# Residual, output and gate transfers on GpSimd's queue, quadrant rows loaded by halves a step ahead, and a looser chain for the right operands' sums

## The chip, the cores and the metric

The kernel runs on one core of a Trainium2 chip. The metric is the device time of one execution in microseconds (us). Before the change it is 2142.83 us, the median of three runs (2140.28 to 2150.28).

The engines are named as the profile names them: PE (TensorE, the matmuls), DVE (VectorE), ACT (ScalarE), POOL (GpSimd) and SP (SyncE, which here only issues DMAs). Each engine takes its instructions strictly in order. A DMA is issued by an instruction in the queue of one engine; if that instruction has to wait, everything behind it in the same queue waits too.

## The reference

The input x has shape (4, 1024, 2048), in float32. One block of a network with modulated layer norms is computed:

```python
x = x + ga * s4_convolution(layernorm(x) * (1 + ca) + sa)
x = x + gb * ffn(layernorm(x) * (1 + cb) + sb)
# ffn(h) = h @ W.T + bias + sum over 16 experts of a rank-16 update
```

The gates and shifts (sa, ca, ga, sb, cb, gb) come from a small matmul of the conditioning vector, and the 16 low-rank updates are merged into W on the chip. What the change touches is the second line: a 4096 x 2048 by 2048 x 2048 product, with its layer norm ahead of it and its gate, bias and residual behind it.

## The kernel before, in words

**First part, 0 to some 911 us.** The convolution is done as Toeplitz matmuls, block of 128 rows by block of 128 rows (32 blocks). Its result goes to the HBM tensor `x1d` (32 blocks of 128 x 2048), and each block's mean and scale go to `ln2`. Beside it the merged weights are written to HBM as `wcd`: seven right operands, each number as a pair of float16 (high and low part).

**Second part, `Ffn`, from 911 us to the end.** Four batches `s`, each of eight row blocks, so 1024 x 2048 by 2048 x 2048. Each batch product is taken apart by Strassen-Winograd into seven products of half size, in the order `ORDER = (0, 1, 5, 2, 6, 4, 3)`; `m` is the place in that order. A product runs as eight groups in `plain` (L1107): one group fills one PSUM bank of 128 x 512 with 24 matmuls (two halves of the inner dimension, four blocks, three pairs of high and low parts). From batch 1 on, the four products in `INNER` are taken apart once more in `twice` (L1130), into seven smaller products with right operands `wid`.

**Left operands.** `quad_steps` (L797) makes one quadrant (two row blocks, 1024 columns): `load` fetches two 128 x 1024 tiles `xr` from `x1d` by SP's queue (L805), `norm` normalizes them on ACT (L811), and four `turn` steps transpose them on PE into PSUM tiles `tp` (L818) and bring them back on ACT with the modulation (L821). The pool `xr` has two places, so one quadrant is in flight. `sum_steps` adds quadrants on DVE, and `piece_steps` and `inner_steps` cut the results into float16 pairs `lf` (ACT makes the high part, L860 and L875; DVE the low part, L861 and L876).

**Right operands of the second level.** In batch 0 alone, `combine_steps` (L898) runs 16 times, four times in each of the places m = 0, 2, 3 and 4 (`CBM`). Each time it loads four 128 x 2 x 512 pieces `cbi` of `wcd` (SP, L907), adds high and low parts on POOL (`whole`, L913: tiles `cbf` a, b, c), forms four sums on DVE (L928, L934, L936, L941), and for each sum calls `out`: ACT writes the high part of `cbo` (L917), DVE the low part (L918), SP stores it to `wid` (L919). `cbo` has two places, `cbi` has four.

**Results.** `outer` (L1082) takes a finished PSUM bank into accumulators on DVE or ACT. In the products 1, 4 and 3 (`FIN`) results become final, and `finish` (L1069) is called, in product 4 twice for each group: DVE adds the gated bias to the residual tile `xo` (L1075), multiplies by the gate (L1076) and adds (L1077); SP stores `xo` to `out` (L1079); then `fetch` (L1062) loads the residual that is four places further on into the place that has just been stored (L1065). `xo` has four places. `gates` (L1045) loads the gate and the gated bias for 1024 columns, 512 KB each, by SP's queue (L1050), and `scale` multiplies the gate once (L1056).

**What sets the order.** `side` (L957) gives every one of these steps a due time in groups, 0 to 8 within a product; `tick` calls the steps that are due after each group. A scheduler then moves instructions within each engine's queue by its own estimate of the times, but each engine runs them in the order that comes out. Weights `w` (1 MB each) are loaded by SP's queue too (L786).

Of the kernel before, what the change touches and what calls it, by code (L numbers as in the profile page):

```python
# [757 lines left out]
class Ffn:  # L758
# [38 lines left out]
    def quad_steps(self, s, u, hr, hc):  # L797

        nc, k = self.nc, self.k
        xs = []  # L800

        def load():
            for rb in range(2):
                x = self.pl["xr"].tile([P, D // 2], F32, tag="xr", name="xr")
                nc.sync.dma_start(out=x, in_=k.x1d[8 * s + 4 * u + 2 * hr + rb][:, ds(1024 * hc, 1024)])  # L805
                xs.append(x)

        def norm():
            for rb, x in enumerate(xs):
                r = 8 * s + 4 * u + 2 * hr + rb  # L810
                nc.scalar.activation(x, x, AF.Identity, bias=k.ln2[:, r, 0:1], scale=k.ln2[:, r, 1:2])  # L811

        def turn(c0):
            t = self.quad(f"{hr}{hc}{u}")
            tp = k.tps.tile([P, 2, 2, P], F32, tag="t", name="tp2")
            for c in range(2):
                for rb in range(2):
                    nc.tensor.transpose(tp[:, c, rb], xs[rb][:, ds(P * (c0 + c), P)], k.ident)  # L818
            for c in range(2):
                j = HC * hc + c0 + c  # L820
                nc.scalar.activation(  # L821
                    t[:, c0 + c], tp[:, c], AF.Identity, bias=k.sb[:, j, s : s + 1], scale=k.cb[:, j, s : s + 1]
                )

        return [load, norm] + [lambda c0=c0: turn(c0) for c0 in range(0, HC, 2)]

    def sum_steps(self, i, u):
        tt = self.nc.vector.tensor_tensor
# [69 lines left out]
    def combine_steps(self, i, k):  # L898

        nc = self.nc  # L900
        tt, gt = nc.vector.tensor_tensor, nc.gpsimd.tensor_tensor
        f, src = {}, {}

        def load(*names):
            for n in names:
                t = self.pl["cb"].tile([P, 2, 512], F16, tag="i", name="cbi", bufs=CBI)
                nc.sync.dma_start(out=t, in_=self.wcd_row(i, n, k))  # L907
                src[n] = t

        def whole(tag, n):  # L910
            f[tag] = self.pl["cb"].tile([P, 512], F32, tag=f"f{tag}", name="cbf")
            t = src.pop(n)
            gt(f[tag], t[:, 0], t[:, 1], ADD)  # L913

        def out(c, t):
            hl = self.pl["cb"].tile([P, 2, 512], F16, tag="o", name="cbo", bufs=2)
            nc.scalar.copy(hl[:, 0], t)  # L917
            tt(hl[:, 1], t, hl[:, 0], SUB)  # L918
            STQ(nc).dma_start(out=self.wid[i][c - 3][:, k], in_=hl)  # L919

        def s0():
            load("11", "12")
            whole("a", "11")
            whole("b", "12")

        def s1():
            f["c"] = self.pl["cb"].tile([P, 512], F32, tag="fc", name="cbf")
            tt(f["c"], f["b"], f["a"], SUB)  # L928
            out(4, f["c"])
            load("22", "21")  # L930
            whole("c", "22")

        def s2():
            tt(f["b"], f["c"], f["b"], SUB)  # L934
            out(6, f["b"])
            tt(f["a"], f["b"], f["a"], ADD)  # L936
            out(5, f["a"])
            whole("c", "21")

        def s3():  # L940
            tt(f["c"], f["c"], f["a"], SUB)  # L941
            out(3, f["c"])

        return [s0, s1, s2, s3]

    def wcd_row(self, i, n, k):
        kh, q = int(n[0]) - 1, int(n[1]) - 1
# [1 line left out]

    def begin(self):  # L950

        q = [self.quad_steps(0, 0, 0, 0), self.quad_steps(0, 1, 0, 0), self.quad_steps(0, 0, 0, 1)]
        p = [self.piece_steps(ORDER[0], u) for u in range(2)]
        self.nextq = self.quad_steps(0, 1, 0, 1)
        return q[0] + p[0] + q[1] + q[2] + p[1] + self.nextq[:1]

    def side(self, s, m):  # L957

# [5 lines left out]
            for j, f in enumerate(fs):  # L964
                out.append((t + j // n, f))

        def quad(st, t):
            put(t, st[1:2])
            put(t + 1, st[2:], 2)

        def quads(s, todo):

            n = 8 / max(len(todo), 1)
            for j, x in enumerate(todo):
                st = self.quad_steps(s, *x)
                t = j * n
                out.append((t + 0.01 if j else 0, st[0]))
                out.append((t + n / 3, st[1]))
                out.append((t + 2 * n / 3 - 0.1, st[2]))
                out.append((t + 2 * n / 3, st[3]))  # L980
                out.append((t + n - 0.2, st[4]))
                out.append((t + n - 0.1, st[5]))

        if (s, m) == (0, 0):
            c, d = self.quad_steps(0, 0, 1, 0), self.quad_steps(0, 0, 1, 1)
            self.nextq, e = d, self.nextq
            quad(e, 0)
            put(2, c[:1])
            quad(c, 3)
            put(5, d[:1])  # L990
            put(6, d[1:2])
            put(7, d[2:4], 2)
        elif (s, m) == (0, 1):
            c, d = self.quad_steps(0, 1, 1, 0), self.quad_steps(0, 1, 1, 1)
            put(0, self.nextq[4:] + c[:1], 3)
            quad(c, 1)
            put(3, d[:1])
            quad(d, 4)
        elif s + 1 < NB:
            quads(s + 1, {  # L1000
                4: ((0, 0, 1), (1, 0, 1)), 5: ((0, 0, 0), (1, 0, 0), (0, 1, 0)), 6: ((1, 1, 0), (0, 1, 1), (1, 1, 1))
            }.get(m, ()))

        if s:
            for u in range(2):
                if m == 0:
                    put(1 + 2 * u, self.sum_steps(5, u))
                    put(6 + u, self.sum_steps(2, u))
                elif m in (3, 4):
                    put(0.5 + u, self.sum_steps(ORDER[m + 1], u))  # L1010
        elif m in (1, 3, 4):
            for u in range(2):
                put(1 + 5 * u, self.sum_steps(ORDER[m + 1], u), 2)
                if m == 1:
                    put(3.5 + 4 * u, self.sum_steps(2, u))

        if m + 1 < len(ORDER) or s + 1 < NB:
            i = ORDER[(m + 1) % len(ORDER)]
            now, then = inner(s, ORDER[m]), inner(s + (m == 6), i)
            for u in range(2):  # L1020
                st = self.inner_steps(i, u) if then else self.piece_steps(i, u)
                if then:
                    ts = [E * (p + 2) + 0.1 for p in range(7)] if now else [2, 4, 6, 6.5, 8, 9.2, 10.4]
                elif now:
                    ts = [E * (2 + (4 * u + j) // 2) + 0.1 for j in range(4)]
                else:
                    ts = [2 + 4 * u + j // 2 for j in range(4)]
                for t, f in zip(ts, st):
                    if t >= 8:
                        self.later.append((t - 8 + 0.02, f))  # L1030
                    else:
                        out.append((t, f))
        if s == 0 and m in CBM:
            n = CBM.index(m)
            for k in range(4):
                for j, f in enumerate(self.combine_steps(INNER[n], k)):
                    out.append((2 * k + (j - 1) / 2 if k or j else 0, f))
        return sorted(out, key=lambda x: x[0])

    def open_slots(self):  # L1040
# [4 lines left out]
    def gates(self, hc):  # L1045
        k = self.k
        t = self.pl["g"].tile([P, 2, 1024], F32, tag="gb", name="gb")
        for i in range(2):
            src = k.gbd[i][self.s][ds(1024 * hc, 1024)]
            self.nc.sync.dma_start(out=t[:, i], in_=src.partition_broadcast(P))  # L1050
        self.gb, self.gbias = t[:, 0], t[:, 1]
        self.raw = True

# [6 lines left out]
        return x[8 * self.s + 4 * u + 2 * hr + rb][:, ds(1024 * hc + 512 * q, 512)]  # L1060

    def fetch(self, n):  # L1062
        while self.nxo < min(n, len(self.fin)):
            x = self.pl["o"].tile([P, 512], F32, tag="o", name="xo")
            self.nc.sync.dma_start(out=x, in_=self.at(self.k.x1d, *self.fin[self.nxo]))  # L1065
            self.xo[self.nxo] = x
            self.nxo += 1

    def finish(self, key, t):  # L1069
# [6 lines left out]
        v.tensor_tensor(t, t, self.gb[:, sl], MUL)  # L1076
        v.tensor_tensor(x, x, t, ADD)  # L1077
        out = self.k.io["out"].rearrange("(r p) d -> r p d", p=P)
        STQ(self.nc).dma_start(out=self.at(out, *key), in_=x)  # L1079
        self.fetch(n + AHEAD)  # L1080

    def outer(self, i, u, rb, q, ps):  # L1082
# [108 lines left out]
    def run(self):  # L1191
        self.w0, self.ne, self.raw = 0, 0, False
        for s in range(NB):
# [5 lines left out]
            self.nxo, self.xo = 0, {}  # L1199
            for m, i in enumerate(ORDER):  # L1200
                side = self.side(s, m)
                if m == 0:
                    self.fetch(AHEAD)
                if m in (0, 6):
                    self.gates(0)
                elif m == 4:
# [17 lines left out]
BLOCK = {0: (0, 0), 1: (0, 1), 2: (1, 1)}  # L1224
BANK = {0: "x", 1: "x", 4: "y", 2: "y", 5: "z", 6: "z", 3: "z"}
CBM = (0, 2, 3, 4)
CBI = 4
FIN = {1: (("a", (0, 0)),), 4: (("a", (0, 1)), ("b", (1, 1))), 3: (("b", (1, 0)),)}
LEFT = {0: "00", 1: "01", 5: "s2", 2: "01", 6: "00", 4: "10", 3: "11"}
Q1 = ("000", "001", "010", "011", "100", "101")  # L1230
# [30 lines left out]
def net(ctx: ExitStack, tc: tile.TileContext, io):  # L1261
# [165 lines left out]

    def early():
        right.close()
        for name, bufs in (("q", 1), ("xr", 2), ("l", LR)):  # L1430
            pr[name] = pool(p2, "p2" + name, bufs, "right")

    calls = [0]
# [146 lines left out]
```

## Time and profile before

| what | value |
|---|---|
| median of three runs | 2142.83 us |
| the profiled execution, its own time | 2143.21 us |
| its span in the trace | 2141.4 us |
| granted TensorE clock, mean | 0.976 |
| second part: first matmul at, last matmul at | 910.9 us, 2135.6 us |
| one PSUM group of 24 matmuls | 5.18 us |
| DMA instructions on SP's queue in one execution: xr, xo, out, gb | 64, 128, 128, 24 |
| DMA instructions on POOL's queue | 28, all before 141 us |

The profile of an execution has a page and a trace. The page gives the busy time of each engine, the costliest groups of instructions with what ended the idle time before them, and the chain of waits that ended last. The trace answers for any stretch: busy time of each engine, the granted clock (PEclk, 1.00 is full speed), the share of time in which the DMA engines were busy, and who waited for whom. In the list of waits a line reads "engine, tile and line that waited <- engine, tile and line that it waited for: us in total, times, longest". A name such as SPq stands for the queue of an engine, where DMAs are issued.

### The profile page before, as it was taken

How to read it: one execution, taken by the hardware profiler on the slowest of the kernel's cores; microseconds unless marked ns; L12 is line 12 of the kernel's file. 1: busy time of each engine (PE TensorE's matmuls, PEld its weight loads, DVE VectorE, ACT ScalarE, POOL GpSimd, SP SyncE). 2: the span in 40 equal slices, each digit the busy share in tenths (PEclk: the TensorE clock that was granted, in tenths of full speed). 3: DMA queues.
4: the chain of work that ended last, by engine and by line, in shares of the span. 5: the costliest groups of instructions: out<-in, count | busy, mean ns of one | idle time of the engine just before them, and what ended most of it. 6: DMA issues, size and time to landing. Idle time of an engine off the chain costs nothing.

```text
span 2141.4 us, 28492 instructions
## 1 busy us (share of the span) xinstructions
PE 2019.2 (94%) x10557; PEld 968.2 (45%) x10557; DVE 1617.6 (76%) x2798; ACT 950.4 (44%) x1754; POOL 116.5 (5%) x117
## 2 busy tenths in 40 slices
PE   6898999999999999989996989999899999999998
PEld 2343444444444455544443444445444444444444
DVE  5437798888979898558976778866787857778666
ACT  1324876666766686744324442224351244412210
POOL 1020000000000000032443000000000000000000
PEclk7898999999999999999998999999999999999999
DMA  9796858888986674478767876666885667766665
GB/s 405 305 377 255 326 219 336 341 330 315 338 315 232 226 263 163 155 269 276 259 241 248 274 266 217 251 208 229 275 286 198 235 211 266 270 208 244 200 220 190
DMA packets 139129, 559.16 MB, mean 261 GB/s; under 512 B 15456, under 2 KB 15984, under 8 KB 93166
## 3 DMA queue, kind: packets, MB, share of 16 engines
q1 hardware_dynamic: 137392, 553.06, 72.0%
q10 hardware_dynamic: 526, 2.63, 0.3%
q8 instruction: 83, 1.36, 0.3%
q0 software_dynamic: 1072, 1.65, 0.2%
q14 instruction: 56, 0.46, 0.1%
HBM read 443.63 MB, written 113.65 MB: 260 GB/s over the span
## 4 chain that ended last, share of the span: by engine, by line
PE 34%; DMA 9%; DVE 5%; issue 2%; ACT 1%; POOL 1%; SPq 0%; ACTq 0%; DVEq 0%; POOLq 0%
PE f L1119 13%; PE fz L1147 8%; PE fy L1147 6%; PE fx L1147 5%; DMA out<-xo 3%; DMA wid<-cbo 2%; DMA xr<-x1d 2%; DMA xo<-x1d 2%; PE tp L818 1%; POOL cbf L913 1%; DVE cbo L918 1%; DVE e L1102 1%; DVE e L1076 1%; DVE xo L1077 1%; DVE lf L876 0%
## 5 line engine op out<-in xcount | busy, mean ns | idle before, releaser
L1119 PE MATMUL f<-w,lf 128*128 128x512 f16 x3072 | 683.1, 383 | 2.1 <-DMA w<-wcd 2.1
L1119 PEld LDWEIGHTS <-lf 128*128 128x128 f16 x3072 | 303.3, 99 | 359.0 <-issue 13.4
L676 PEld LDWEIGHTS <-hc 128*128 128x128 f16 x2304 | 212.3, 98 | 215.1 <-issue 53.4
L1147 PEld LDWEIGHTS <-lf 128*128 128x128 f16 x2016 | 197.3, 98 | 235.0 <-issue 0.7
L676 PE MATMUL ya<-kh,hc 128*128 128x512 f16 (+3 forms) x768 | 203.9, 329 | 7.0 <-ACT qs L691 6.7
L676 PE MATMUL yb<-kh,hc 128*128 128x512 f16 (+3 forms) x768 | 200.9, 326 | 1.9 <-DVE we L503 1.1
L1147 PE MATMUL fz<-w,lf 128*128 128x512 f16 x864 | 192.8, 379 | 0.4 <-DVE ca L1165 0.4
L676 PE MATMUL ya<-kh,hs 128*128 128x512 f16 (+3 forms) x768 | 189.9, 326 | 2.2 <-DVE we L503 1.2
L676 PEld LDWEIGHTS <-hs 128*128 128x128 f16 x1152 | 106.1, 98 | 111.3 <-issue 26.5
L641 ACT ACTIVATE xt<-xt,cas 128x128 f32<-128x128 f32 x448 | 141.1, 393 | 10.2 <-DVE cas L587 10.2
L811 ACT ACTIVATE xr<-xr,ln 128x1024 f32<-128x1024 f32 x64 | 79.3, 1241 | 147.8 <-DMA xr<-x1d 147.5
L1075 DVE TENSOR_TENSOR xo<-xo,gb 128x512 f32<-128x512 f32 x128 | 87.9, 703 | 69.4 <-DMA xo<-x1d 55.6
L319 PE MATMUL modps<-wm,sct 128*32 128x512 f32 x768 | 119.3, 656 | 16.2 <-DMA wm<-in_wmod 8.9
L1147 PE MATMUL fx<-w,lf 128*128 128x512 f16 x576 | 129.5, 379 | 0.0
L818 PE MATMUL tp<-ident,xr 128*128 128x128 f32 x512 | 77.8, 289 | 53.7 <-ACT xr L811 35.7
L1147 PE MATMUL fy<-w,lf 128*128 128x512 f16 x576 | 128.2, 379 | 0.0
L676 PE MATMUL ya<-kl,hc 128*128 128x512 f16 (+3 forms) x384 | 126.1, 329 | 0.0
L676 PE MATMUL ya<-kl,hs 128*128 128x512 f16 (+3 forms) x384 | 125.1, 326 | 0.0
L676 PE MATMUL yb<-kl,hc 128*128 128x512 f16 (+3 forms) x384 | 125.1, 326 | 0.0
L875 ACT CAST lf<-t 128x512 f16<-128x512 f32 x72 | 44.3, 617 | 179.5 <-PE f L1119 84.9
L913 POOL TENSOR_TENSOR cbf<-cbi 128x512 f32<-128x512 f16 x64 | 93.8, 1467 | 294.3 <-DVE xo L1075 146.1
L818 PEld LDWEIGHTS tp<-ident,xr 128*128 128x128 f32 x512 | 61.9, 147 | 77.6 <-ACT xr L811 42.3
(380 smaller groups left out, 2765.8 us busy)
## 6 DMA issues: line engine op xcount, KB each, us to landing
w<-wcd SPq DMA_DIRECT2D x100, 1024.0 KB
wm<-in_wmod SPq DMA_DIRECT2D x96, 1024.0 KB
w<-wid SPq DMA_DIRECT2D x48, 1024.0 KB
x<-in_x SPq DMA_DIRECT2D x32, 1024.0 KB
x1d<-y SPq DMA_DIRECT2D x32, 1024.0 KB
xr<-x1d SPq DMA_DIRECT2D x64, 512.0 KB
xo<-x1d SPq DMA_DIRECT2D x128, 256.0 KB
out<-xo SPq DMA_DIRECT2D x128, 256.0 KB
```

The lines of the kernel that those rows point to most:

```text
L319: self.last = self.nc.tensor.matmul(self.modps[32 * g : 32 * g + 32, :], self.sct[:, j].rearrange("p r b -> p (r b)"), w[:, ds(512 * g, 512)],
L641: nc.scalar.activation(xt[:, k], src, AF.Copy, scale=cas[:, k : k + 1])
L676: nc.tensor.matmul(pf[:, o:512], h, self.kf[f][z][:, ds(k0, 512 - o)], start=first, stop=(i == last and (x, z) == (1, 0)), skip_group_chec ...
L811: nc.scalar.activation(x, x, AF.Identity, bias=k.ln2[:, r, 0:1], scale=k.ln2[:, r, 1:2])
L818: nc.tensor.transpose(tp[:, c, rb], xs[rb][:, ds(P * (c0 + c), P)], k.ident)
L875: nc.scalar.copy(hl[:, :, 0, :], src)
L913: gt(f[tag], t[:, 0], t[:, 1], ADD)
L918: tt(hl[:, 1], t, hl[:, 0], SUB)
L1075: v.tensor_tensor(x, x, self.gbias[:, sl], ADD)
L1076: v.tensor_tensor(t, t, self.gb[:, sl], MUL)
L1119: nc.tensor.matmul(ps, l[:, c, x, :], w[:, c, y, :], start=(n == 0), stop=(n == 23), skip_group_check=True)
L1147: nc.tensor.matmul(ps[name], l[:, k, x, :], w[:, k, y, :], start=(first and n == 0), stop=(n == 11), skip_group_check=True,)
```

## The change

Four things change, all in `Ffn`.

1. The gate loads (`gates`), the residual loads (`fetch`) and the result stores (`finish`) are issued by POOL instead of SP. In batch 0 the first residuals are fetched at m = 1 instead of m = 0, no more than eight of them until m = 5.
2. A quadrant is handled in two halves of 512 columns: four places of 128 x 512 for `xr` instead of two of 128 x 1024, eight smaller `norm` instructions for a pair of quadrants where there were four, and each half's load is due one half's time before its norm. The due times of all quadrants are set anew.
3. `combine_steps` is split into loads and sums that are due with the combination before, and three steps after them. A fourth tile `d` holds one of the sums, the results of one step are converted two at a time (both high parts, then both low parts), and `cbo` now takes its places from the pool `o` of four, which it shares with `xo`.
4. Some due times of sums and pieces in batch 0 move.

No arithmetic is added or left out.

```diff
@@ quad_steps
-        def load():
-            for rb in range(2):
-                x = self.pl["xr"].tile([P, D // 2], F32, tag="xr", name="xr")
-                nc.sync.dma_start(out=x, in_=k.x1d[8 * s + 4 * u + 2 * hr + rb][:, ds(1024 * hc, 1024)])
+        def load(h):
+            for rb, r in enumerate(rows):
+                x = self.pl["xr"].tile([P, 512], F32, tag="xr", name="xr")
+                nc.sync.dma_start(out=x, in_=k.x1d[r][:, ds(1024 * hc + 512 * h, 512)])
...
-        return [load, norm] + [lambda c0=c0: turn(c0) for c0 in range(0, HC, 2)]
+        return [
+            [lambda h=h: load(h), lambda h=h: norm(h), lambda h=h: turn(h, 0), lambda h=h: turn(h, 2)] for h in range(2)
+        ]
@@ combine_steps
-        def out(c, t):
-            hl = self.pl["cb"].tile([P, 2, 512], F16, tag="o", name="cbo", bufs=2)
-            nc.scalar.copy(hl[:, 0], t)
-            tt(hl[:, 1], t, hl[:, 0], SUB)
+        def high(c):
+            hl = self.pl["o"].tile([P, 512], F32, tag="o", name="cbo").bitcast(F16)
+            hl = hl.rearrange("p (y n) -> p y n", y=2)
+            nc.scalar.copy(hl[:, 0], f[WHERE[c]])
+            f[c] = hl
+        def low(c):
+            hl = f[c]
+            tt(hl[:, 1], f[WHERE[c]], hl[:, 0], SUB)
             STQ(nc).dma_start(out=self.wid[i][c - 3][:, k], in_=hl)
...
+        def sums():
             whole("a", "11")
             whole("b", "12")
             whole("c", "22")
+        def first():
+            tt(new("d"), f["b"], f["a"], SUB)
+            high(4)
             tt(f["b"], f["c"], f["b"], SUB)
+            high(6)
+            low(4)
+            low(6)
+        def second():
             tt(f["a"], f["b"], f["a"], ADD)
+            high(5)
+            tt(f["d"], f["d"], f["a"], SUB)
+            high(3)
+            low(5)
+            low(3)
-        return [s0, s1, s2, s3]
+        before = [lambda: load("11", "12", "22"), lambda: load("21"), sums]
+        return before, [first, lambda: whole("d", "21"), second]
@@ side
+        def halves(hs, t, d, loaded=0):
+            for j, h in enumerate(hs):
+                if j >= loaded:
+                    add(t + (j - 1) * d, h[0])
+                add(t + j * d + 0.1, h[1])
+                add(t + (j + 0.55) * d, h[2])
+                add(t + (j + 0.9) * d, h[3])
...
+        elif s + 1 < NB and m in (4, 5, 6):
...
+            d = 4 / len(todo)
+            halves(quads(s + 1, *todo), d, d)
@@ gates, fetch, finish
-            self.nc.sync.dma_start(out=t[:, i], in_=src.partition_broadcast(P))
+            self.nc.gpsimd.dma_start(out=t[:, i], in_=src.partition_broadcast(P))
...
-            self.nc.sync.dma_start(out=x, in_=self.at(self.k.x1d, *self.fin[self.nxo]))
+            self.nc.gpsimd.dma_start(out=x, in_=self.at(self.k.x1d, *self.fin[self.nxo]))
...
-        STQ(self.nc).dma_start(out=self.at(out, *key), in_=x)
+        self.nc.gpsimd.dma_start(out=self.at(out, *key), in_=x)
@@ run
-                if m == 0:
-                    self.fetch(AHEAD)
+                self.cap = 8 if s == 0 and m < 5 else len(self.fin)
+                if (s, m) in ((0, 1), (0, 5)) or s and m == 0:
+                    self.fetch(self.nxo + AHEAD)
@@ net
-        for name, bufs in (("q", 1), ("xr", 2), ("l", LR)):
+        for name, bufs in (("q", 1), ("xr", 4), ("l", LR)):
```

## The prediction

> **What bounds the kernel now.** I read the page's first part, then PE's waits in the second part, then a table of stretches, and last the waits of the two queues that stand behind PE's waits.
>
> ```profile
> PE 2019.2 (94%) x10557; PEld 968.2 (45%) x10557; DVE 1617.6 (76%) x2798; ACT 950.4 (44%) x1754; POOL 116.5 (5%) x117
> ```
>
> PE is the bound, and the question is what it loses. From 910.9 to 2136.2 us (1225.3) it has 5088 group matmuls, at 5.18 us for 24 (the chain's long rows: 192 in 41.44), so 1098.2 us, and 464 transposes (512 less the 48 made before 911), at 0.87 us for eight, so 50.5. The rest, 76.6 us, is all that a change of this part can win. PE's waits from 820 us on:
>
> ```profile
> PE tp L818 <- ACT xr L811: 35.7, 18, 5.5
> PE tp L818 <- ACT 010_8586 L821: 14.9, 1, 14.9
> PE tp L818 <- ACT 011_8911 L821: 2.7, 1, 2.7
> PE f L1119 <- DMA w<-wcd: 2.1, 1, 2.1
> ```
>
> These make 55.4 us, and all but the last are transposes that wait for ACT. The table of stretches (start and end, length, busy time of PE and of PEld, DVE, ACT, POOL, then PEclk, DMA share, GB/s) shows where:
>
> ```profile
> 952.40:1005.00 52.60, 43.25 (x199) 21.09 (x197) 38.42 (x46) 24.97 (x42) 13.37 (x10) 0.90 0.84 281
> 1113.00:1182.00 69.00, 50.25 (x225) 24.02 (x224) 47.30 (x65) 26.92 (x48) 25.02 (x18) 0.85 0.70 244
> 1182.00:1262.00 80.00, 70.48 (x350) 35.47 (x349) 56.40 (x91) 33.20 (x53) 0.00 (x0) 0.96 0.77 263
> 1317.00:1440.00 123.00, 123.00 (x571) 55.74 (x570) 92.84 (x142) 27.73 (x46) 0.00 (x0) 1.00 0.61 212
> 1481.00:1572.00 91.00, 84.37 (x422) 43.20 (x421) 70.22 (x108) 40.05 (x66) 0.00 (x0) 0.98 0.78 264
> 1774.00:1866.00 92.00, 85.66 (x429) 43.77 (x427) 72.18 (x111) 41.26 (x68) 0.00 (x0) 0.98 0.78 261
> ```
>
> The clock is 1.00 where PE never waits (1317 to 1440) and lower in the stretches with waits, so a wait costs more than its length. I take the waits of a stretch plus PE's busy time by what PEclk lacks:
> - A, 905 to 1010 (m = 0 and 1 of batch 0): waits 11.2, clock 43.25 x 0.10 = 4.3; 15.5.
> - B, 1025 to 1182 (the right operands' sums): waits 20.8, clock 50.25 x 0.15 = 7.5, and 85.95 x 0.02 = 1.7 before 1113; 30.0.
> - C, 1182 to 1262 (the last two products of batch 0): 9.5 + 2.8 = 12.3.
> - D and E (the same of batches 1 and 2): 6.6 + 1.7 and 6.3 + 1.7; 8.3 and 8.0.
>
> Together 74.1 of the 76.6.
>
> **C, D, E: rows that come late.** SP's own waits in E:
>
> ```profile
> SPq L1065 <- DMA out<-xo: 37.7, 18, 6.5
> SPq L1079 <- DVE xo L1077: 22.7, 16, 4.5
> ```
>
> That is 60 of 92 us in which SP's queue stands at a residual load (its place is still being stored) or at a store (DVE is not done). The `xr` loads and the weights are behind it. In D it is 61 of 91, in C 52 of 80. All PE waits of these three are for the norm of `xr`, and ACT in turn waits for the load. The change takes both from SP; what remains there in E are waits of 3.5 us (L805) and 0.4 (L786). The load is now due 1.33 + 0.1 groups ahead of its norm (7.4 us) where three quadrants share a product, instead of 0.89 (4.6 us). In the chain, `xr` takes 5.7 to 8.3 us from issue to landing, for pairs of 512 KB; the halves carry half of that. 7.4 us is enough for most. Of 28.6 us I take 23 as won, and leave 5.6 for loads that meet two weights.
>
> The smaller norms cost nothing on the path: ACT needs 0.62 us for 128x512 (the cast of L875), twice that is 1.24, what one norm takes now (1241 ns). SP gets 64 `xr` issues more (0.38 us each, 24 us over 1225) and loses 280. If ACT were no longer idle half of the time, the norms would count.
>
> **B: the sums.** ACT's waits from 1100 to 1182:
>
> ```profile
> ACT cbo L917 <- DMA wid<-cbo: 27.6, 9, 4.5
> ACT cbo L917 <- DVE cbf L934: 8.1, 3, 2.8
> ```
>
> `cbo` has two places, so ACT stands until a store has landed; the eviction of `tp` that PE wants is behind it on ACT (14.9 us). POOL's sums show the pace: six rounds from 1073.22 to 1149.12, so 12.65 us a round, where the products give 41.4 / 4 = 10.4. With four places a round no longer waits for its own stores. Its longest chain is then, from the rows: two POOL sums 3.1 (1.96 apart, then 1.15), DVE 0.69, ACT 0.62, DVE 0.69, POOL 1.54, DVE twice 0.69, ACT 0.62, DVE 0.69; 9.3 us with no queueing. DVE is busy 81% between 1025 and 1113 (71.24 of 88), so I take 11. The order of the changed program still puts all 16 rounds ahead of the first eviction that PE needs late in m = 4, six groups into it: 2 x 41.4 + 31 = 114 us after m = 2 begins, for 11 rounds. At 11 us they end 7 us late, at 9.3 in time, at 12.65 25 us late, as now. With its share of clock that leaves 10 of 30: 20 won, with ends 0 and 30.
>
> **A: places shared.** In the changed order the last two `cbo` of m = 0 stand on ACT, in m = 1, behind the store of the first finished tile (and the next four behind those of tiles four and later), with norms and evictions queued behind them. The trace has no such wait. The first store lands about one group (5.18), five DVE instructions (3.4) and one store (4.5) after m = 1 begins, 13 us; PE wants the norm behind it after three groups, 15.5 us. It just holds, but if the residual comes 5 us late, PE waits for 3, and the next `cbo` waits for its predecessor's store on top. Nearest rows on either side: the 11.2 us of waits here could all go, or a 14.9 us wait like that of B could come. I take 4 won, since SP is relieved here too (16.5 + 11.9 us of its waits between 905 and 1182).
>
> **POOL's queue instead of SP's.** What POOL pays to issue and how long a transfer takes:
>
> ```profile
> kb<-kd POOLq DMA_DIRECT2D x1, 1024.0 KB, 9.6
> gsd<-rkg POOLq DMA_DIRECT2D x24, 12.0 KB, 5.1
> gm<-gsd POOLq DMA_DIRECT2D x1, 288.0 KB, 7.4
> ```
>
> Issue takes 0.51 to 0.74 us there (eight `gsd` in 4.09, `kd` 0.74). At two tiles a group, in product 4, that is 4 x 0.74 = 3.0 us of 5.18: POOL is not the bound. The landing matters more. For comparison, SP's stores and loads on the chain in D:
>
> ```profile
> 1490.71 6.82 DMA out<-xo
> 1497.55 3.75 DMA xo<-x1d
> 1515.92 3.04 DMA out<-xo
> 1518.97 3.01 DMA xo<-x1d
> ```
>
> A place of `xo` is used again after two groups in product 4, 10.36 us. A turn is a store, a load, and about 2.5 us of DVE and of queue order: with SP's 3.0 to 6.8 and 3.0 to 3.75 it is 8.5 to 13. With 5.1 twice it is 12.7, and DVE falls behind by 2.3 us every two groups, three times over, 7 us; with 7.4 twice 17.3, 21 us. PE is covered by five PSUM banks, four groups or 20.7 us: DVE already waits 55.6 us for `xo` and the PE list has nothing of it. I take 5.5, near the 12 KB row, because a separate queue doesn't stand behind 1 MB weights, and charge 2 us. The last store pays 0.4 us more to issue and lands up to 2 later: 2 us. Together 4, with ends at 0 and 70.
>
> POOL's 94 us of sums lie in the same queue as stores that wait for DVE, in m = 1 of batch 0 only; I leave that in A.
>
> The Trainium skill speaks against this move. Its page "DMA: Bandwidth & Descriptors", section "Issuing engine by pattern", gives simple loads and stores to Sync and calls the GpSimd path slower; the section "Anatomy of one DMA" has 2.0 us plus the bytes at 436 GB/s, an estimate of 2.6 us for 256 KB. No row here is that short; by it the turn would be 7.7 us and DVE would lose nothing.
>
> The page "SBUF — State Buffer", section "Who interferes with whom", says that a DVE instruction in a two-port mode locks GpSimd out of writing descriptors. The trace shows a tile instruction at that double pace only in L1056 (128x1024 in 0.75 us, twelve in this part), so by the rule at most 9 us in all.
>
> **Sum.** 23 + 20 + 4 - 4 = 43 from the profiled execution's 2143.2: 2100 us. That execution lies 0.4 above the median of the three, so the number stands for the median as well. Half a per cent, 10.7 us, is about what a measurement of this kernel can tell from no change.
>
> **Rivals.**
> - *The sums stay slow* (20%). DVE, 81% busy, sets the 12.65 us and not the stores; or ACT's wait in A takes its place. Then 23 - 4 remain: 2124 us. For it: ACT also waits for L934 (8.1). Against it: the stores are the longest wait.
> - *POOL's transfers are slow* (15%), the one that ends slower. If a store and a load of 256 KB each take 9.6 us as `kb` did, a turn is 21.7 us, DVE falls 34 us behind in each product 4, PE waits for the 13 beyond its banks, and the product after it (one tile a group, four places, 21.7 of 20.7 us) never gives the lag back: 34 less a little each batch, 25 or so x 4 = 100, less the 43 + 4 without POOL's price: some 2196. Up to about 7.4 us each nothing of this shows; from there on it decides. For it: landing rows of 5.1 to 9.6. Against it: those ran while 16 engines were near full (first slices 9 7 9 6), here the share is 0.6 to 0.8.
> - *Nothing changes* (10%): `xr` was late for the DMA engines' load (0.78 in D and E) rather than for SP, and the sums stay as they are: 2140.
>
> **Chances.** The forecast has 55%, with its own range of 2084 (B and C to E wholly won) to 2118. Faster by over 0.5%: 55 + 20 = 75%, less 1 for the upper edge; within: 10 and a little; slower: 15. For 8 in 10 the range leaves out the slow rival and the best few per cent: 2084 to 2150.
>
> **What will show it.** C to E: no PE wait on L812, SP's queue without waits on `out`. B: POOL's rounds at 11 us or less, PEclk near 1.00 between 1113 and 1182. A: ACT's waits of `cbo` on DMA `out<-xo`. POOL: store and load of `xo` near 5.5 us each. Wrong would be: DVE waits on `xo` that grow above 100 us with PE waiting for banks, or rounds still at 12 us.

## The result, and the profile after

The changed kernel takes 2274.05 us (median, 2266.6 to 2275.13) against 2145.94 us for the kernel before in the same measurement (2140.28 to 2150.28): ratio 1.0591, 95% interval 1.0554 to 1.0628. The prediction, 2100 us and at most 2150, was wrong in sign. The profiled execution took 2275.06 us, with a span of 2273.3 us and a mean granted clock of 0.954 (before 0.976).

The first part of the page (busy time and share of the span):

```profile
PE 2043.0 (90%) x10557; PEld 975.8 (43%) x10557; DVE 1626.5 (72%) x2798; ACT 963.5 (42%) x1818; POOL 266.9 (12%) x397
```

PE does the same 10557 instructions, in 23.8 us more of busy time (the lower clock), and sits idle more. PE's waits from 820 us on:

```profile
PE tp L819 <- ACT 110_9252 L823: 42.4, 3, 17.8
PE fz L1165 <- DVE cb L1180: 33.6, 3, 13.9
PE tp L819 <- ACT 100_9068 L823: 22.2, 3, 8.9
...
PE tp L819 <- ACT xr L812: 7.2, 7, 2.6
```

The whole list comes to 145.7 us, against 56.8 before. The waits for `xr` fell from 35.7 to 7.2, as the change meant. Three others, each met three times, are new. Batch 1's three stalls in the table of stretches (columns as in the prediction):

```profile
1580.00:1600.00 20.00, 10.83 (x42) 4.99 (x40) 17.36 (x29) 7.08 (x13) 6.46 (x13) 0.76 0.68 219
1620.00:1640.00 20.00, 11.18 (x51) 5.97 (x50) 16.04 (x24) 6.66 (x13) 3.80 (x7) 0.78 0.65 229
1740.00:1760.00 20.00, 6.07 (x20) 2.26 (x19) 12.46 (x21) 0.62 (x1) 0.54 (x1) 0.68 0.44 177
```

PE works 6 to 11 of 20 us there, and the clock drops to 0.68 to 0.78. The end is late too: from the last matmul to the end of the span it is 21.9 us (2251.4 to 2273.3), before 5.4. Waits (88.9 more), clock (23.8) and tail (16.5) make 129 of the 131.9 us between the spans.

Next the waits of DVE, and the wait of POOL's queue that answers to SP's in the prediction:

```profile
DVE xo L1093 <- DMA xo<-x1d: 199.4, 72, 9.1
DVE gb L1074 <- DMA gb<-gbd: 56.2, 11, 13.0
```

```profile
POOL xo L1083 <- DMA out<-xo: 365.1, 100, 9.1
```

DVE waits 199.4 us for the residual instead of 55.6. POOL stands 3.65 us on average until a store has landed, before it can load into that place; SP stood 2.06 (206.3 over 100). Yet the transfers are not long in the median. The DMA issues (last number: us from issue to landing):

```profile
xo<-x1d POOLq DMA_DIRECT2D x128, 256.0 KB, 3.6
out<-xo POOLq DMA_DIRECT2D x128, 256.0 KB, 3.9
```

How this reaches PE is seen in batch 1. POOL's timeline (start, duration, line, operation, count; in brackets the wait before and what ended it):

```profile
1530.86 1.15 POOL L1097 DMA_DIRECT2D out<-xo  x2 [108.94 <-DVE xo L1095]
...
1544.06 1.08 POOL L1097 DMA_DIRECT2D out<-xo  x2
1554.22 0.54 POOL L1083 DMA_DIRECT2D xo<-x1d  x1 [9.08 <-DMA out<-xo]
...
1591.04 1.15 POOL L1097 DMA_DIRECT2D out<-xo  x2
...
1729.93 0.54 POOL L1083 DMA_DIRECT2D xo<-x1d  x1 [7.53 <-DMA out<-xo]
...
1736.19 0.54 POOL L1068 DMA_DIRECT2D gb<-gbd  x1 [0.18 <-issue]
```

In product 4 the stores go two by two, and POOL stands 9.08 us for this pair, where the median landing is 3.9. What ran beside it: SP's timeline, and how the queues shared the 16 DMA engines from 1549 to 1553 us (packets, MB, share of the engines' time):

```profile
1542.16 2.91 SPq L786 DMA_DIRECT2D w<-wcd  x2
```

```profile
q1 hardware_dynamic: 264, 1.21, 73.3%
q0 software_dynamic: 133, 0.41, 25.7%
```

q0 carries 81.36 MB in this execution and 1.65 MB in the one before, so it is POOL's; q1 has SP's transfers. Two weights of 1 MB were issued just ahead of the pair, rows followed from 1545.55 on, and while the pair was under way SP's queue had three quarters of the engines. Two residual loads of POOL itself (issued from 1542.98 on) were also just ahead of it. DVE's timeline:

```profile
1575.98 0.69 DVE L1093 TENSOR_TENSOR xo<-xo,gb 128x512 f32<-128x512 f32 x1 [5.25 <-DMA xo<-x1d]
...
1591.26 0.69 DVE L886 TENSOR_TENSOR t<-001_8437 128x512 f32<-128x512 f32 x1
...
1744.86 0.75 DVE L1074 TENSOR_SCALAR gb<-gb,fs_i 128x1024 f32<-128x1024 f32 x1 [13.04 <-DMA gb<-gbd]
```

ACT's, and PE's:

```profile
1591.98 0.62 ACT L879 CAST lf<-t 128x512 f16<-128x512 f32 x1 [21.51 <-DVE t L886]
...
1593.22 1.00 ACT L823 ACTIVATE 100_9068<-tp,sb,cb 128x256 f32<-128x256 f32 x2
```

```profile
1594.27 0.47 PE L819 MATMUL tp<-ident,xr 128*128 128x128 f32 x1 [8.93 <-ACT 100_9068 L823]
...
1756.25 7.67 PE L1165 MATMUL fz<-w,lf 128*128 128x512 f16 x24 [13.93 <-DVE cb L1180]
```

Read from the top: DVE stands at the residual, so the sum `t` (L886), behind it on DVE, comes late; ACT's cast of `t` waits 21.5 us for it; the eviction L823 is behind the cast on ACT, and PE wants it for its next transposes. No PSUM bank of the products is in this chain. The second stall is of the same kind (ACT's cast of `u` waits 13.3 us for DVE, the eviction L823 follows it). The third is the gate: its load was issued at 1736.2, after POOL had stood 7.5 and 4.5 us at two residual loads, and was in place 8.7 us later. DVE stood 13 us at the scaling, with the additions behind it (L1180) that empty PE's banks.

### The profile page after: what moved, and what is told of

Read it like the earlier page. It is cut to its first block, busy times and chain, and to the rows that moved or that the text cites. A ratio compares the mean times of both kernels' runs of the same rounds, so it can differ in the third digit from the quotient of the medians.

```text
span 2273.3 us, 28757 instructions
## 1 busy us (share of the span) xinstructions
PE 2043.0 (90%) x10557; PEld 975.8 (43%) x10557; DVE 1626.5 (72%) x2798; ACT 963.5 (42%) x1818; POOL 266.9 (12%) x397
## 3 DMA queue, kind: packets, MB, share of 16 engines
q0 software_dynamic: 25008, 81.36, 10.3%
## 4 chain that ended last, share of the span: by engine, by line
DMA 18%; issue 17%; PE 14%; DVE 13%; POOL 3%; ACT 1%; SPq 0%; POOLq 0%; DVEq 0%; ACTq 0%
DMA out<-xo 10%; PE fz L1165 4%; DMA xo<-x1d 3%; PE fy L1165 2%; PE f L1137 2%; PE ya L676 2%; PE fx L1165 2%; DMA cbi<-wcd 2%; DVE cbo L930 1%; DMA gb<-gbd 1%; DVE e L1094 1%; POOL xo L1083 1%; DMA wid<-cbo 1%; PE yb L676 1%; DVE e L1120 1%
## 5 line engine op out<-in xcount | busy, mean ns | idle before, releaser
L1093 DVE TENSOR_TENSOR xo<-xo,gb 128x512 f32<-128x512 f32 x128 | 87.2, 690 | 221.4 <-DMA xo<-x1d 199.4
L1165 PE MATMUL fz<-w,lf 128*128 128x512 f16 x864 | 200.6, 389 | 40.8 <-DVE cb L1180 33.6
L819 PE MATMUL tp<-ident,xr 128*128 128x128 f32 x512 | 82.4, 296 | 95.1 <-ACT 110_9252 L823 42.4
L812 ACT ACTIVATE xr<-xr,ln 128x512 f32<-128x512 f32 x128 | 102.2, 812 | 133.7 <-DMA xr<-x1d 133.7
L1097 POOL DMA_DIRECT2D out<-xo x128 | 70.0, 547 | 576.5 <-DVE xo L1095 571.8
```

The costliest lines, as they stand in the source:

```text
L819: nc.tensor.transpose(tp[:, c, rb], xs[h, rb][:, ds(P * (c0 + c), P)], k.ident)
L1093: v.tensor_tensor(x, x, self.gbias[:, sl], ADD)
L1097: self.nc.gpsimd.dma_start(out=self.at(out, *key), in_=x)
L1165: nc.tensor.matmul(ps[name], l[:, k, x, :], w[:, k, y, :], start=(first and n == 0), stop=(n == 11), skip_group_check=True,)
```

## The experiments

Where no ratio is given, there is a single time and no interval; the kernel before took 2146 to 2151 us in the same measurements. Where nothing else is said, the edit is to the changed kernel.

**The queue, or the rest.** First all three transfers back on SP, then the reverse: the kernel before with nothing but the queue changed.

```diff
-            self.nc.gpsimd.dma_start(out=t[:, i], in_=src.partition_broadcast(P))
+            self.nc.sync.dma_start(out=t[:, i], in_=src.partition_broadcast(P))
...
-            self.nc.gpsimd.dma_start(out=x, in_=self.at(self.k.x1d, *self.fin[self.nxo]))
+            self.nc.sync.dma_start(out=x, in_=self.at(self.k.x1d, *self.fin[self.nxo]))
...
-        self.nc.gpsimd.dma_start(out=self.at(out, *key), in_=x)
+        self.nc.sync.dma_start(out=self.at(out, *key), in_=x)
```

> The changed kernel with residual loads, output stores and gate loads back on SP; the half quadrants, their due times and the looser chain of sums stay. Queue theory (POOL's queue takes store, wait for its landing, load, next store in one order, so DVE waits 199 us for the residual and ACT and PE behind it): the 199.4 us of DVE waits for xo fall to 60 or less, and the time is 2100 to 2150, the upper end if the rows stand behind the residual on SP again. Order theory (the new order of rows, pieces and evictions on ACT makes PE's transposes late whatever queue is used): 2230 or more, with the 95 us of PE idle ahead of the transposes still there. Sums theory (the looser chain, with its stores in the residual's four places, is what got slower): in between, with PE's waits gathered in batch 0 and none in the later batches.

Measured: 2147.69 us, ratio to before 0.9991 (0.9974 to 1.0007). SP's waits for a place ahead of a weight load, in the products that are not split in seven, first with all on SP, then in the changed kernel:

```profile
SPq L786 <- PE f L1137: 8.7, 9, 2.1
```

```profile
SPq L786 <- PE f L1137: 219.5, 42, 17.7
```

With all on SP the queue stands 194.2 us at residual loads and 217.2 at stores, and a weight of these products, held back behind them, seldom has to wait for its place as well. With these off SP, the weights are at the head of the queue early and go out as soon as PE has freed a place.

> The kernel before with only the queue changed: residual loads, output stores and gate loads on GpSimd's queue, whole quadrants, old due times and old chain of sums. Queue theory: the loss is nearly all here, 2220 to 2280, DVE waits for xo near 200 us instead of 55.6. Order theory and sums theory: the queue costs little, 2110 to 2150, DVE waits for xo under 100 us.

Measured: 2256.58 us, ratio 1.0515 (1.0481 to 1.0548). The queue alone makes 107 of the 126 us that the changed kernel loses against its version on SP, and the rest of the change is worth nothing on SP. The order theory falls: with whole quadrants and the old due times the same stalls are there. DVE's wait, and PE's longest, in the kernel with only the queue changed:

```profile
DVE xo L1075 <- DMA xo<-x1d: 151.4, 61, 8.3
```

```profile
PE tp L818 <- ACT 111_9572 L821: 43.4, 3, 14.7
```

With all on SP, PE's longest wait from 820 on, and ACT's longest for `cbo` between 1025 and 1190, are:

```profile
PE tp L819 <- ACT xr L812: 31.1, 14, 6.2
```

```profile
ACT cbo L925 <- DVE cbf L939: 37.2, 7, 8.1
```

The rows are late again, and the chain of sums now waits for DVE where it waited for stores.

**One transfer at a time.** Only the gate loads back on SP (the first pair of lines above); only the stores; only the residual loads.

> The changed kernel with only the eight gate loads back on SP. If the gate loads behind the stores are the main cause (gate theory): below 2170. Queue theory: only PE's wait of the fz groups for DVE's L1180 (33.6 us) and DVE's 56.2 us for gb go, with the clock some 40 us: 2225 to 2250, DVE waits for xo near 190 us still. Order theory: as the changed kernel but for those 33.6: about 2240.

Measured: 2226.57 us, DVE's wait for `xo` 217.2. PE's wait for L1180 halves (16.5), and no stall of it is longer than 5.3 us (13.9 in the changed kernel): having the gates on POOL costs 47 us in all. That is a net figure: SP now stands 139.7 us at the gate loads, for a gate tile that DVE still reads, with the rows behind them, and PE's wait for `xr` is 46.5 us, the largest of all runs here.

> The changed kernel with only the output stores back on SP; residual loads and gates stay on POOL. POOL still waits for a store's landing before the load that takes its place, but no store stands behind that wait. Queue theory in the strict form (it is the one order of stores and loads): DVE waits for xo fall to 100 us or less and the time to 2110 to 2190, even though SP's queue again waits for DVE at each store. If GpSimd's queue itself is the cost (a load on it lands late whatever stands ahead of it): DVE waits for xo stay above 150 us and the time above 2220.

Measured: 2217.31 us, DVE's wait 149.9. Both lie well outside what the queue theory gave (by 27 and 50 us) and just short of the other's 2220 and 150. So the one order of stores and loads on POOL is not the whole cause; that the queue itself is the cost does not follow.

> The changed kernel with only the residual loads back on SP; stores and gates stay on POOL, where nothing waits for a landing any more. Queue theory: DVE's waits for xo fall below 110 us and the time to 2140 to 2190; SP waits for the stores' landing with rows and weights behind it, as in the kernel before (206 us), perhaps longer. Contention theory: the stores on POOL land late, SP waits above 300 us, and the time stays above 2220.

Measured: 2208.03 us, DVE's wait 127.2; SP stood 500.6 us at the stores' landing. Neither theory holds in full: the time is 18 us above the one and 12 below the other, with SP's wait as contention had it. With the loads or with the stores alone on POOL, beside the gates, the loss against 2147.69 is 70 and 60 us.

**Depth and order.** Three fetched ahead instead of four; then five places instead of four.

```diff
-AHEAD = 4
+AHEAD = 3
```

> The changed kernel with the residual fetched three finishes ahead instead of four, so a load on POOL takes the place of the tile finished one step earlier, whose store was issued 2 to 8 us before, and not of the tile whose store has just been issued. Queue theory, now sharper (on one queue each tile pays its own store's landing: 365.1 us over 100 loads, 3.65 us each, plus two issues of 0.55, where product 4 gives a tile every 2.6 us): POOL's wait for out falls below 150 us, DVE's wait for xo from 199 to 110 or less, the time to 2190 to 2225 (the gates' 13.9 us stalls stay). Contention theory (a transfer on GpSimd's queue shares the DMA engines with the weights that SP no longer holds back, and lands late whatever the order): the residual, fetched a step later, comes later still, DVE's wait for xo stays at 190 us or more and the time above 2260.

Measured: 2269.99 us, POOL's wait 367.4, DVE's 207.0.

```diff
-    for name, bufs in (("q2", 1), ("c", 1), ("o", 4), ("e", 1), ("g", 1)):
+    for name, bufs in (("q2", 1), ("c", 1), ("o", 5), ("e", 1), ("g", 1)):
```

> The changed kernel with five places for the residual instead of four and still four fetched ahead: again a load takes the place of the tile finished a step earlier, but nothing is fetched later. Queue theory: as with the later fetch or better, POOL's wait for out below 150 us, DVE's for xo below 100, 2180 to 2215. Contention theory: little moves, above 2250.

Measured: 2264.2 us, POOL's wait 403.9, DVE's for `xo` 166.0, for the gate 93.8. By the numbers contention wins, but the first of the two is no test: the scheduler moves the load up until it stands directly behind the store of its own place, and from product 4 of batch 0 on POOL's order is the changed kernel's, letter for letter. (In the source, finish n fetches tile n + 3 into the place of tile n - 1, not into the place just stored; it is the scheduler that puts each load behind its own place's store, in the kernel before as well.) In the second the load still stands behind its own place's store, one place deeper; the residual is earlier and the gate later.

> Five places and the gate loads on SP, residual and stores on POOL. Queue theory: both causes are gone, what is left is the kernel before without residual on SP: PE waits for DVE-made pieces and for L1180 under 10 us together, rows no longer late: 2120 to 2150. Contention theory: the gates' share only, as with gates on SP alone, 2215 to 2235.

Measured: 2199.73 us, ratio 1.0257 (1.0236 to 1.0277). With the gates away, the fifth place gives 27 us (against the single 2226.57); the time is between the two theories, 50 us from the one and 15 from the other. DVE's wait is 184.6, PE's for `xr` 7.6 instead of 46.5.

To force the order, the load is bound behind the store of the same finish, with five places and four or three ahead:

```diff
-        self.nc.gpsimd.dma_start(out=self.at(out, *key), in_=x)
-        self.fetch(n + AHEAD)
+        put = self.nc.gpsimd.dma_start(out=self.at(out, *key), in_=x)
+        with self.k.tc.issue_after(put.ins):
+            self.fetch(n + AHEAD)
```

> Five places, four fetched ahead, and now the load written into POOL's queue behind the store of the same finish. In the two runs before (three ahead, and five places) the planner had moved each load up to stand directly behind the store of its own place, so that POOL still waited for that landing (367 and 404 us) with the next store behind it: they changed the depth and not the order, and so tell nothing against the queue theory. Here a load waits for a store issued one finish earlier. Queue theory: POOL's wait for out falls from 404 to 150 to 250 us, as finishes in product 4 come in pairs 2.1 us apart; DVE's for xo from 166 to about 110; 2190 to 2240 with the gates still on POOL. Contention theory (transfers land late whatever the order): DVE's wait for xo stays above 150, 2250 or more.

Measured: 2254.11 us, POOL's wait for `out` 17.7, DVE's for `xo` 184.5.

> The same with three fetched ahead, so a load takes the place of the tile two finishes back, whose store has had 5 us or more. Queue theory: POOL's wait for out below 100 us, DVE's for xo below 90, the time 2165 to 2210, what is left being the gates (33.6 us of PE's waits for L1180 in the changed kernel). Contention theory: POOL's wait falls but DVE's for xo stays above 150 us, and the time above 2240.

Measured: 2282.97 us. DVE's wait for `xo`, and POOL's longest:

```profile
DVE xo L1093 <- DMA xo<-x1d: 210.2, 82, 7.8
```

```profile
POOL out L1097 <- DVE xo L1095: 952.1, 116, 113.1
```

> The same with the gate loads on SP. Queue theory: neither cause is left, 2120 to 2155 against 2199.7 with five places and gates on SP but the loads behind their own stores. Contention theory: 2190 to 2210, no change by the order.

Measured: 2274.18 us, ratio 1.0571 (1.0538 to 1.0605), above both expectations; DVE's wait 222.5.

My sharper theory falls here, in the form in which I put it. POOL hardly stands at a landing any more, and DVE waits as long as ever; POOL stands at the stores instead, until DVE has finished a tile, and the next load goes out only then. These edits have a price of their own: a load bound behind store n is for tile n + 3 or n + 2, where the changed kernel had n + 4 there, so they take away lead along with the wait. What they show is that POOL's standing is not needed for the stall: with the lead that is left, the landing of a load (median 4.5 us, longest 11.2 with three ahead) is too long. A load that is free of POOL's standing and keeps its lead was not tried.

**Contention.** Every second weight load of the products that are not split in seven is left out (from batch 1 on the products 1, 4 and 3, in batch 0 all from the third on): 28 of 148. POOL's order is unchanged. Then the same on SP as a control.

```diff
+        if n >= 8 and not twice and t % 2:
+            self.wt[n] = self.wt[n - 1]
+            return
```

> The changed kernel, leaving out every second weight load of the products that are not split in seven (the tile before it is multiplied again, so those products are not the reference's); from batch 1 on the 1 MB loads of products 1, 4 and 3 fall from 12 to 6 a batch. The order of stores and loads on POOL stays the same, letter for letter. Contention theory (in product 4 a pair of stores takes 6 to 9 us to land beside the weights and rows that SP no longer holds back, against 3.9 in the median): stores there land in 3 to 5 us, DVE's wait for xo falls from 199 to 130 or less, and the time to 2170 to 2225. Queue theory (the order alone): within 15 us of 2274, DVE's wait for xo above 180.

Measured: 2210.08 us. The median landing of the stores falls from 3.9 to 3.3 us. DVE's wait:

```profile
DVE xo L1097 <- DMA xo<-x1d: 149.5, 69, 6.3
```

> The control for it: the same weights left out, with residual, stores and gates on SP. Both theories: 2115 to 2150, as SP's queue is relieved a little; if it falls by as much as the other, the weights' traffic costs PE in both and says nothing of POOL.

Measured: 2136.95 us. These weights are worth 64 us with the residual on POOL, at the same order of stores and loads, and 11 on SP, where the scheduler moved some of them. Each of the two is a single time. DVE's wait did not fall to 130, but the time is in the range that contention gave.

**What is left, and a better version.**

> Residual loads and stores on POOL, gates on SP, five places, and every second weight load of the products that are not split left out (the tile before is multiplied again, so these products are not the reference's). It is 2199.7 with all weights. If contention with the weights, the gates behind the stores and the depth of four places are the whole of the loss, it comes to 2135 to 2150 (2137 with half the weights and all on SP). If GpSimd's queue costs more than these by itself, 2165 or more, with DVE's wait for xo above 120 us.

Measured: 2154.25 us, DVE's wait 131.7. The time lies between the two answers, DVE's wait is as the second had it. Against 2136.95 us, with the same weights and all on SP, 17 us are left of the 126 (the tail, 8.5 instead of 5.6, is 3 of them); that control has four places, not five.

> The kernel before, all on SP, with the residual fetched three finishes ahead. If the order of store and load costs on SP as well (206 us of SP's waits for a store's landing, with rows and weights behind them): SP's wait for out falls below 100 us, the 35.7 us of PE's waits for xr by a half, 2120 to 2138. If SP's waits are hidden or the wait for DVE (217 us) merely takes their place: 2140 to 2155.

Measured: 2153.37 us, ratio 1.0034 (1.0016 to 1.0052). SP's wait for `out` falls to 142.9, that for DVE grows from 217.0 to 252.1; PE's for `xr` is 41.2. On SP one wait takes the other's place.

> All three transfers on SP, with the half quadrants and the looser chain, and five places for the residual instead of four (there is room for the fifth only with the new chain, which gives back cbo's two tiles). If what holds the version on SP at 2147.7 is SP's standing for stores (194 us, DVE's wait for xo 101.5) with rows behind it, a fifth place gives some of it back: 2125 to 2143. If the rows are late for the DMA engines' load: 2143 to 2152.

Measured: 2137.75 us, ratio 0.996 (0.9944 to 0.9976): as the first answer had it, and faster than the kernel before by 0.4%. SP's wait for `out` is 149.6, PE's for `xr` 21.6.

> The same with only the gate loads on POOL, where no store or residual load stands ahead of them any more. If the 47 us that the gates cost on POOL in the changed kernel come from standing behind the stores: equal to the version with the gates on SP or up to 10 us faster. If a gate load on GpSimd's queue is slow by itself: 15 to 50 us slower than it.

Measured: 2148.03 us, ratio 1.0005 (0.999 to 1.0021), 10 us behind the version with the gates on SP: between the two answers. Set against the gates' 47 us in the changed kernel, some 37 come from what stands ahead of them; that is an estimate, as the two differences are taken in different kernels. DVE's wait for the gate is no longer (37.7 against 42.1), and where the 10 us are lost was not found.

```diff
-                nc.sync.dma_start(out=x, in_=k.x1d[r][:, ds(1024 * hc + 512 * h, 512)])
+                (nc.gpsimd if s else nc.sync).dma_start(out=x, in_=k.x1d[r][:, ds(1024 * hc + 512 * h, 512)])
```

> The reverse split: residual, stores and gates on SP with five places, and the rows of batches 1 to 3 on POOL, where a load waits only for PE's transposes and nothing else stands in the queue but the sums. If the rows are late for SP's standing: PE's wait for xr falls from 21.6 to 8 us or less and the time from 2137.7 to 2115 to 2132. If a load on GpSimd's queue lands late beside the weights, as the residual did: PE's wait for xr stays or grows, 2137 to 2160.

Measured: 2137.76 us, ratio 0.9953 (0.9926 to 0.9979), the same as with the rows on SP. The rows land late here too (4.9 us in the median, 10.3 at worst), yet PE's wait for `xr` falls by half (10.1); a wait for the eviction of `110_9252` on ACT grows to 19.0.

## Why the prediction was wrong, point by point

**POOL's queue: the step that failed.** It was priced at 4 us and cost 126 with the whole change (2274.05 against 2147.69), 107 alone. The chosen landing was not the mistake: 5.5 us was taken, 3.6 and 3.9 are the medians. Four parts of the step were wrong.
- The turn of a place was put at 12.7 us (landings of 5.1; with the 5.5 taken it is 13.5), with one store's landing in it. In batch 1's product 4 POOL issues eight pairs of stores between 1530.86 and 1591.04, so 8.6 us a pair, and with two pairs to the four places a turn of 17.2; the products give a pair every 5.18. In POOL's order (two stores, their landing, two loads, the next two stores) a turn holds the landings of two pairs, one after the other. On SP the same count gives 13.6 (1479.48 to 1527.19), also more than the prediction's 8.5 to 13: its chain has a load of 5.84 us (at 1508.66) that is not among the four lines shown.
- "PE is covered by five PSUM banks, four groups or 20.7 us". The banks cover the additions of the products, but DVE also makes the sums that ACT cuts into pieces, and ACT also empties the transposes. A late DVE reaches PE through ACT's queue, without a bank in between. Of the sign that was to show the step wrong, one half came: DVE's waits for `xo` went above 100 us (199.4), but PE's waits for banks were not the main ones.
- "a separate queue doesn't stand behind 1 MB weights". It runs beside them. On SP the standing at the residual also held the weights and rows back; off SP they are issued as soon as their places are free (SP's wait for PE ahead of a weight goes from 8.7 to 219.5 us in the products that are not split in seven), and a pair of stores in product 4 can then hold POOL for 9 us. The trace shows both queues on the DMA engines at once, and the two runs with half the weights show that it costs time (64 us against 11). So one median landing was the wrong thing to put into the turn.
- The gate loads were given no price. In POOL's order they stand behind residual loads that wait for landings: 47 us, net of what the rows lose when the gates go back to SP.

The rival "POOL's transfers are slow" had the right sign, but its point of decision (7.4 us for each transfer) was not reached by the medians: a place's turn came to 17 us all the same. Its 2196 was too low: it let the banks cover 21 us of each lag, charged nothing for the gates, and took off 47 us of gains, of which at most the rows' 23 came.

**The last store.** 2 us were charged; the tail grew by 16.5. DVE finishes its last tile 13.5 us after the last matmul, 2.2 before: its lag is paid once more at the end. From there to the end of the span it is 8.3 us instead of 3.2.

**C, D, E.** 23 us for the rows: as far as these waits go the mechanism was right and the size too: from 1182 us on, PE's waits for `xr` were 22.4 before and are 0.7 now. It needs SP's queue free of everything that stands, though: from 1182 on they are 17.2 with all on SP and 38.3 with only the gates there. The smaller norms cost more than was put: 0.81 us each and not 0.62, so ACT spends 102.2 us on them instead of 79.3; no run shows what that is worth.

**B.** 20 us for the sums: the first rival came nearer. With the stores' wait gone, ACT waits for DVE's sums (37.2 and, for L949, 15.9). With all on SP the sums do end earlier (POOL's last one starts at 1156.71, before at 1168.90), but PE's waits for the late eviction only go from 14.9 to 12.2 us. Between 1025 and 1190 PE works 144.16 us with all on SP, against 142.57 before: 1.6 won. With five places it is 149.99, so the number of shared places seems to matter as well.

**A.** 4 us: PE's waits between 905 and 1025 are 13.9 with all on SP, 11.2 before. Nothing was won. The wait at the shared places that was feared is small: ACT stood there 7.8 us once, for a DVE instruction, in the changed kernel, and PE's waits for evictions up to 1025 come to 3.4 us.

**The pages.** The Trainium skill, "DMA: Bandwidth & Descriptors", "Issuing engine by pattern", gives simple loads to Sync. For residual, stores and gates together the runs agree (2147.69 against 2274.05); for the rows they don't show a price (2137.76 against 2137.75). The same page, "Queues, rings and completion order", says that a DMA engine takes packets in turn from the queues that have work. The trace fits that: from 1549 to 1553 us both queues move data (73.3% and 25.7% of the engines' time). So do the runs with half the weights, with a median landing of the stores of 3.9 us with all weights and 3.3 with half; neither shows the turns themselves.

**What stays open.** How the 126 us divide between the landings in series, the weights beside them, the gates and the depth was not found, as the parts act on one another. 17 us remain with gates, depth and half of the weights removed. Whether the rows' loads, the other half of the weights or the longer issue (0.55 us on POOL, 0.33 on SP) make them was not tried.

## What to carry to other kernels

A queue that stands is also a brake: before a waiting transfer is moved off it, ask what the freed queue will now issue beside that transfer, and price the turn with that traffic in flight. Follow a late engine through every in-order queue that uses what it makes, the small side jobs too, before you say that buffers cover it. And look at the order that the scheduler writes, since a shorter prefetch in the source may leave it as it was.

## What the runs showed of the hardware

- A 256 KB transfer on GpSimd's queue landed in 2.3 us at best, 3.9 in the median and 10.3 at worst (stores, changed kernel); its issue took 542 to 564 ns each time, with DVE busy 72% of the span.
- Transfers of SP's and of GpSimd's queue were under way on the 16 DMA engines at the same time (1549 to 1553 us in the changed kernel): 1.21 MB and 0.41 MB, 73.3% and 25.7% of the engines' time.
- GpSimd's queue carried the 256 KB loads of the rows of batches 1 to 3 at no cost in time (2137.76 against 2137.75 us), although they landed in 4.9 us in the median; residual, stores and gates on it cost 107 us. So a transfer on this queue need not cost time. That the difference lies in who waits for it, and with how much lead, is argued and not shown.
